# A macaron transformer kernel: bias and residual sums of the tail moved from TensorE to GpSimd, and left out of the build-time clock's stages

## The chip, the cores and the metric

The kernel runs on one core of a Trainium2 chip. The metric is the device time of one execution in microseconds (us). A core has five instruction queues that run side by side, each strictly in its own order: TensorE (PE, matrix products), VectorE (DVE), ScalarE (ACT), GpSimd (POOL) and SyncE (SP, which issues DMAs). They meet only in semaphores.

## The reference, cut to what matters

The input is 8 sequences of 512 rows by 128 features, float32. The stream `x` of each sequence goes through six layers. A routed expert layer stands first (`s = 0`), then attention (`s = 1`), then a second expert layer (`s = 2`). The last three are here called the tail:

```
x = x + 0.5 * fp6(layernorm(x))                  # called s = 3
x = x + mix(layernorm(x))                        # a gated scan, then a gated feed-forward
x = x + 0.5 * fp6(layernorm(x))                  # called s = 5

fp6(u):  out = quantized(u) @ quantized(weight).T + bias
mix(u):  u = u + scan(sigmoid, tanh of products of rmsnorm(u))
         return u + (silu(gate(rmsnorm(u))) * up(rmsnorm(u))) @ W_out.T
```

Two sums of this matter here. The first is `+ bias` in fp6, which reaches the stream halved. The second is the `u +` of mix's last line: the stream gets `x + u + product`.

## The kernel before, in words

Every sequence ("batch" `b`) has one resident tile `X[b]`, 128 partitions by 4 x 128 values (L270). The program is written by Python generators. Each yields after a stage, and a driver decides whose next stage is written down, so that the order on every engine's queue is fixed when the program is built.

The class `Clock` (L67 to L174) guesses times for that purpose. Each engine call is logged by `_Logged.noted` (L187 to L190; this is why the profile shows nearly every instruction as L190). `took` (L82) gives a guessed duration: a GpSimd operation on 512 values per partition is 0.2 + 0.0018 x 512 = 1.12 us. `account` (L100) adds a stage's operations up, moves each engine's "free" time on, and returns when the stage is over; after a GpSimd operation it adds 0.5. A generator's next stage is written only once that moment has come (`is_ready`, L143; `finish`, L164).

The order of the work: expert layer 0, then attention over the 8 batches one after another with the expert layer 2 of finished batches woven in (`drive`, L146), and last a `finish` over what remains (the last call of `tile_macaron_kernel`). The remainder is the 19 expert tiles of group 1 (batches 5, 6, 7), the gathers that combine the results of group 0 and of group 1 (`moe_combine`, L960, indirect DMAs issued by GpSimd), and the eight tails (`tail`, L1439), four in flight at most. A batch's tail starts when its gathers are done. The gathers of group 1 read what all its tiles have stored, so they start after the last of these tiles.

A tail on the engines:

- `fp6` (L1296): statistics on DVE, a power on GpSimd (`power`, L405), the normed row on ACT, quantization on DVE (`quantized`, L1249: one maximum, then six operations on 512 values), four transposes on PE (`tp_xd`), the bias product on PE (L1311), a copy of the transposes to SBUF on ACT (L1317), four products with the weight (L1320) and the sum into `X[b]` on DVE (L1326). The bias product multiplies a row of ones with the bias row and starts the accumulation in the PSUM bank `yp`.
- `mix` (L1332): statistics, powers, three products of 512 columns (`pgd`, `pgg`, `pgv`), tanh on ACT, a scan on DVE, transposes (`tp_h`), `u` completed on DVE (the tile `um_m`), the second norm, six products (`gt`, `up`), and the output. There the identity product (L1426) puts `u` into the bank `yo`, twelve products add to it, and DVE adds the bank to `X[b]` (L1437).

In attention, `roped` (L1027) makes queries and keys. It has one GpSimd sum of the same size, 128 x 512, per rope (`ta_q`, `ta_k`).

A float32 matmul of 512 columns shows as two records in the profile.

Of the kernel before, what the change touches and what calls it, by code (L numbers as in the profile page):

```python
# [9 lines left out]
F32 = mybir.dt.float32  # L10
# [3 lines left out]
ALU = mybir.AluOpType  # L14
# [3 lines left out]
P = 128  # L18
S = 512
NT = S // P  # L20
# [5 lines left out]
NGF = 3  # L26
# [40 lines left out]
class Clock:  # L67
# [32 lines left out]
    def account(self, ready, chained=True):  # L100

        end, last = ready, None
        product = ready
        for engine, op, out, args in self.log:
            took = self.took(engine, op, out, args)
            dep = end if chained and engine != last else ready
            if not chained and engine != "tensor":
                dep = product
            at = max(self.free[engine], dep) + took
            self.free[engine] = at  # L110
            if engine == "tensor":
                product = at
            end, last = (at if chained else max(end, at)) + 0.1, engine
            if op == "indirect_dma_start":
                end = at
            elif engine == "gpsimd":
                end += 0.5
        self.log.clear()
        return end
# [120 lines left out]
def kernel(  # L240
# [17 lines left out]
    nc = tc.nc  # L258
    ck = Clock(nc)
# [4 lines left out]
    cpool = ctx.enter_context(tc.tile_pool(name="const", bufs=1))  # L264
# [8 lines left out]
    X = []  # L273
    for b in range(nb):
        xt = xpool.tile([P, NT, P], F32, tag=f"x{b}", name=f"x{b}")
# [22 lines left out]
    ident = cst[:, C_ID : C_ID + P]  # L298
# [9 lines left out]
    ones = cpool.tile([P, P], F32, tag="ones", name="ones")  # L308
# [41 lines left out]
    ):  # L350
        rest_of_consts[name] = (const_tile(f"{name}_s", ap, dtype), ap)
    rope_s, wattn_s, future_s, vec_s, wq8_s, wmix_s, wout_s = (t for t, _ in rest_of_consts.values())
    bq_s = cpool.tile([P, P], F32, tag="bq_s", name="bq_s")
    half_vec = cpool.tile([P, 2], F32, tag="half_vec", name="half_vec")

    clear_rows(1)
    for t, ap in rest_of_consts.values():
        nc.sync.dma_start(out=t, in_=ap)
    nc.sync.dma_start(out=bq_s, in_=bq.partition_broadcast(P))

    nstat, vpad = [], []
    for k in range(2):
# [3 lines left out]
    def clear_for_attention():  # L366

        for t in nstat:
            ck.gpsimd.memset(t, 0.0)
            yield  # L370


        for t in vpad:
            ck.gpsimd.memset(t, 0.0)
            yield
            ck.gpsimd.memset(by_pair(t)[:, :, :, DK : DK + 1], 1.0)
            yield
        ck.gpsimd.tensor_scalar_mul(half_vec[:, 0:1], vec_s[:, V_BG : V_BG + 1], 0.5)
        ck.gpsimd.tensor_scalar_mul(half_vec[:, 1:2], vec_s[:, V_BD : V_BD + 1], 0.5)
        yield  # L380

    def by_pair(t):

        v = t.rearrange("p (a k) (y d) -> p a (k y) d", k=2, d=16)
        return v[:, :, 0:4:3, :]
# [4 lines left out]
    def bank(name):  # L390
        return p_ps.tile([P, S], F32, tag="ps", name=name)
# [5 lines left out]
    def turned(src, name):  # L397

        tp = bank(f"tp_{name}")
        for t in range(NT):  # L400
            ck.tensor.transpose(tp[:, ts(t, P)], src[:, t, :], ident)
        return tp


    def power(v, eps, name):  # L405
        rs = small.tile([P, NT], F32, tag="rs", name=f"rs_{name}")
        ck.vector.tensor_scalar_add(rs, v, eps)
        yield
        ck.gpsimd.tensor_tensor(rs, rs, mhalf[:, 0:NT], ALU.pow)
        yield  # L410
        return rs

    def moments(src, name, mv=None):
        st = small.tile([P, NT, ck.vector.BN_STATS_DIM], F32, tag="bst", name=f"st_{name}")
        if mv is None:
            mv = small.tile([P, NT, ck.vector.BN_AGGR_DIM], F32, tag="bmv", name=f"mv_{name}")
        for t in range(NT):
            ck.vector.bn_stats(out=st[:, t, :], in_=src[:, t, :])
        for t in range(NT):
            ck.vector.bn_aggr(out=mv[:, t, :], in_=st[:, t, :])  # L420
        return mv

    def normed_act(src, mv, rs, name, tag="u"):

        nb_ = small.tile([P, NT], F32, tag="nbias", name=f"nb_{tag}_{name}")
        ck.vector.scalar_tensor_tensor(nb_, mv[:, :, 0], -1.0, rs, ALU.mult, ALU.mult)
        yield
        u = wk.tile([P, NT, P], F32, tag=tag, name=f"{tag}_{name}", bufs={"um": 4, "row": 4}.get(tag, 2))
        for t in range(NT):
            ck.scalar.activation(  # L430
                u[:, t, :], src[:, t, :], AF.Identity,
                scale=rs[:, t : t + 1], bias=nb_[:, t : t + 1],
            )
        yield "product"
        return u
# [813 lines left out]
    def quantized(src, g, name, slots=None):  # L1249

        am = small.tile([P, 16], F32, tag="q_am", name=f"am_{name}")[:, 0:g]
        ck.vector.tensor_reduce(am, src, AX.X, ALU.max, apply_absolute_value=True)
        sc = small.tile([P, 16], F32, tag="q_sc", name=f"sc_{name}")[:, 0:g]
        ck.vector.tensor_scalar(sc, am, 1.0 / 7.5, 1e-30, ALU.mult, ALU.max)
        rs = small.tile([P, 16], F32, tag="q_rs", name=f"rs_{name}")[:, 0:g]
        ck.vector.reciprocal(rs, sc)
        yield
        if slots:
            yield from slots.take()

        def work(k, dtype=F32):
            t = wk.tile([P, 16, FB], dtype, tag=f"a{k}", name=f"q{k}_{name}")
            return t[:, 0:g, :]

        def along(t):
            return t.unsqueeze(2).to_broadcast([P, g, FB])

        y = work(0)
        ck.vector.tensor_tensor(y, src, along(rs), ALU.mult)

        im, t = work(1, I32), work(2)
        ck.vector.tensor_scalar(
            im, y.bitcast(I32), 0x7F800000, 0x00400000, ALU.bitwise_and, ALU.bitwise_or
        )
        m = im.bitcast(F32)
        ck.vector.tensor_scalar(m, m, 1.5, 2.0**20, ALU.max, ALU.mult)
        yield

        ck.vector.scalar_tensor_tensor(t, y, -(2.0**-21), m, ALU.add, ALU.add)
        ck.vector.tensor_tensor(t, t, m, ALU.subtract)  # L1280
        ck.vector.tensor_tensor(y, t, along(sc), ALU.mult)
        yield
        return y

    wd_t = cpool.tile([P, P], F32, tag="wd_t", name="wd_t")
# [10 lines left out]
    def fp6(b, s):  # L1296

        name = f"{s}_{b}"
        mv = moments(X[b], name)
        rs = yield from power(mv[:, :, 1], 1e-5, name)  # L1300
        u = yield from normed_act(X[b], mv, rs, name, tag="um")

        xd = yield from quantized(
            u.rearrange("p t (g k) -> p (t g) k", k=FB), S // FB, name, rounding
        )
        yield from turning.take()
        tp = turned(xd.rearrange("p (t g) k -> p t (g k)", t=NT), f"xd_{name}")
        rounding.give()

        yp = bank(f"yp_{name}")  # L1310
        ck.tensor.matmul(  # L1311
            yp.rearrange("p (t d) -> p t d", t=NT), ones[0:1, :],
            bq_s[0:1].unsqueeze(1).to_broadcast([1, NT, P]), start=True, stop=False,
        )
        yield
        xt = wk.tile([P, S], F32, tag="uT", name=f"uT_xd_{name}")
        ck.scalar.copy(xt, tp)  # L1317
        yield "product"
        for t in range(NT):
            ck.tensor.matmul(  # L1320
                yp[:, ts(t, P)], xt[:, ts(t, P)], wd_t, start=False, stop=(t == NT - 1)
            )
        turning.give()
        yield
        xb = X[b].rearrange("p t d -> p (t d)")
        ck.vector.scalar_tensor_tensor(xb, yp, 0.5, xb, ALU.mult, ALU.add)  # L1326
# [5 lines left out]
    def mix(b):  # L1332
# [19 lines left out]
        u = wk.tile([P, NT, P], F32, tag="um", name=f"um_m_{b}", bufs=4)  # L1352
# [14 lines left out]
        def gate(i, bias, half, n):  # L1367
            pg = bank(f"pg{n}_{b}")
            ck.tensor.matmul(pg, wmix_s[:, ts(i, P)], xnt, start=True, stop=True)
            t = wk.tile([P, S], F32, tag=("qm", "ka", "qa")[i], name=f"gt{n}_{b}", bufs=(2, KBUFS, 2)[i])  # L1370
            ck.scalar.activation(t, pg, AF.Tanh, bias=bias, scale=half)
            return t


        d = gate(2, half_vec[:, 1:2], 0.5, "d")
# [15 lines left out]
        uf = u.rearrange("p t d -> p (t d)")  # L1391
# [22 lines left out]
        for f in range(NGF):  # L1414
# [6 lines left out]
            ck.vector.tensor_tensor(sg, sg, pu, ALU.mult)  # L1421
            sgs.append(sg)
            yield

        yo = bank(f"yo_{b}")
        ck.tensor.matmul(yo, ident, uf, start=True, stop=False)  # L1426
        for t in range(NT):
            for f in range(NGF):
                ck.tensor.matmul(
                    yo[:, ts(t, P)], sgs[f][:, ts(t, P)], wout_s[:, f, :],  # L1430
                    start=False, stop=(t == NT - 1 and f == NGF - 1),
                )
        gating.give()
        feeding.give()
# [141 lines left out]
```

## Time and profile before

| | |
|---|---|
| three runs | 1114.25, 1116.26, 1118.13 us (median 1116.26) |
| profiled execution | 1195.04 us, of which the span of the records is 1193.3 us |
| mean granted TensorE clock in it | 0.92 |
| busy in the span | PE 995.5, DVE 683.6, ACT 494.9, POOL 472.8 us |
| the chain that ended last, by engine | PE 57%, DVE 16%, issue 7%, POOL 5%, ACT 4% |
| bias products (`yp<-bq_s,ones`) | 32 records, 23.5 us busy, the first at 932.6, the last at 1186.2 us |
| identity products (`yo<-um_m,cst`) | 16 records, 8.8 us busy, 994.7 to 1168.6 us |
| POOL sums of 128 x 512 (`ta_q`, `ta_k`) | 16, all in attention, 1266 and 1281 ns on average |
| the gathers of group 1 | POOL, 1044.7 to 1099.7 us |

The table is from one profiled execution and from three runs without a profile. A "span" counts from the first record to the last. The busy time of an engine is the union of its records. In the timelines each row is a start, a duration, the engine and the operation as output<-inputs, then shapes; brackets hold the idle time just before and who ended it. In the windows, a row is a stretch of time with the busy us of each engine and the number of instructions, then the clock that was granted to TensorE (1.00 is full speed).

### The profile page before, as it was taken

How to read it: one execution, taken by the hardware profiler on the slowest of the kernel's cores; microseconds unless marked ns; L12 is line 12 of the kernel's file. 1: busy time of each engine (PE TensorE's matmuls, PEld its weight loads, DVE VectorE, ACT ScalarE, POOL GpSimd, SP SyncE). 2: the span in 40 equal slices, each digit the busy share in tenths (PEclk: the TensorE clock that was granted, in tenths of full speed). 3: DMA queues.
4: the chain of work that ended last, by engine and by line, in shares of the span. 5: the costliest groups of instructions: out<-in, count | busy, mean ns of one | idle time of the engine just before them, and what ended most of it. 6: DMA issues, size and time to landing. Idle time of an engine off the chain costs nothing.

```text
span 1193.3 us, 20637 instructions
## 1 busy us (share of the span) xinstructions
PE 995.5 (83%) x6753; PEld 693.5 (58%) x6753; DVE 683.6 (57%) x2550; ACT 494.9 (41%) x1135; POOL 472.8 (40%) x627
## 2 busy tenths in 40 slices
PE   3351699799998998998998999999968898887795
PEld 2350598687774545555554567766957666554453
DVE  6040133355556888867676856532523775788755
ACT  1210233233354646464545444444312475544651
POOL 3647202331127658745363523214025452174210
PEclk9995799799999999989898889999979899995897
DMA  9542477487658001000000153334555550011000
GB/s 291 181 148 82 129 230 233 152 267 209 191 155 237 21 15 35 25 10 17 4 19 1 37 159 102 122 112 133 151 156 175 155 150 20 27 41 40 0 10 27
DMA packets 122363, 127.34 MB, mean 107 GB/s; under 512 B 9616, under 2 KB 103696, under 8 KB 122256
## 3 DMA queue, kind: packets, MB, share of 16 engines
q1 hardware_dynamic: 114064, 109.22, 30.4%
q0 software_dynamic: 8192, 16.79, 4.4%
q8 instruction: 54, 0.88, 0.3%
q14 instruction: 53, 0.43, 0.1%
HBM read 79.58 MB, written 46.40 MB: 106 GB/s over the span
## 4 chain that ended last, share of the span: by engine, by line
PE 57%; DVE 16%; issue 7%; another core or an unknown queue 7%; POOL 5%; ACT 4%; DMA 3%; SPq 1%; POOLq 0%; DVEq 0%; ACTq 0%
PE yp L190 13%; PE hp L190 11%; PE sa L190 9%; PE av L190 6%; PE sb L190 5%; DVE q L190 3%; POOL y L190 3%; DVE seen L190 2%; DVE x L190 2%; DVE st L190 1%; PE gt L190 1%; ACT um L190 1%; DMA y<-rows_out,at 1%; PE xp L190 1%
## 5 line engine op out<-in xcount | busy, mean ns | idle before, releaser
L190 DVE CUSTOM_DVE_ANT_0 seen<-sa,future_s 128x128 f32<-128x128 f32 (+3 forms) x512 | 225.2, 486 | 98.3 <-PE sb L190 70.5
L190 ACT ACTIVATE pm<-sb 128x512 f32<-128x512 f32 (+1 forms) x384 | 182.0, 525 | 205.0 <-PE sb L190 179.7
L190 PE MATMUL yp<-wx,hs 128*128 128x128 f32 x1472 | 207.3, 284 | 53.6 <-ACT hs L190 29.2
L190 ACT ACTIVATE hs<-hp,wx 128x256 f32<-128x256 f32 x276 | 119.8, 470 | 313.5 <-PE hp L190 188.4
L190 PEld LDWEIGHTS yp<-wx,hs 128*128 128x128 f32 x1472 | 193.1, 198 | 74.4 <-issue 34.5
L190 PE MATMUL sb<-qa,ka 32*128 32x512 f32 (+3 forms) x1024 | 222.7, 488 | 6.7 <-DVE nstat L190 4.8
L190 PE MATMUL sa<-ka,qz 32*128 32x384 f32 (+3 forms) x1024 | 211.3, 484 | 3.7 <-DVE nstat L190 2.5
L190 PE MATMUL hp<-xt,wx 128*128 128x256 f32 x736 | 204.5, 403 | 9.8 <-DVE g L190 5.3
L190 POOL TENSOR_SCALAR_AFFINE_SELECT pm<-pm 128x256 f32<-128x256 f32 x256 | 100.8, 409 | 240.3 <-ACT pm L190 229.3
L190 POOL DMA_INDIRECT y<-rows_out,at x128 | 134.9, 1054 | 137.7 <-DMA rows_out<-yo 77.9
L190 DVE TENSOR_SCALAR hs<-hp,wx 128x256 f32<-128x256 f32 x92 | 44.5, 483 | 214.6 <-ACT hs L190 196.6
L190 PEld LDWEIGHTS hp<-xt,wx 128*128 128x128 f32 x736 | 133.8, 201 | 39.7 <-issue 15.6
L190 PEld LDWEIGHTS sa<-ka,qz 32*128 32x128 f32 x1024 | 106.7, 194 | 71.8 <-issue 23.4
L190 PEld LDWEIGHTS sb<-qa,ka 32*128 32x128 f32 x1024 | 103.8, 190 | 30.5 <-DVE nstat L190 7.6
L190 POOL TENSOR_TENSOR rs<-rs,mhalf 128x4 f32<-128x4 f32 (+2 forms) x44 | 53.2, 1211 | 165.8 <-DVE rs L190 126.1
L190 PE MATMUL av<-pm,vpad 128*32 128x512 f32 (+3 forms) x1024 | 96.3, 472 | 2.8 <-POOL pm L190 2.6
L190 POOL DMA_INDIRECT by_stretch<-um,sat x64 | 64.3, 1005 | 30.6 <-DVE nt L190 13.4
L190 DVE SCALAR_TENSOR_TENSOR x<-y,g,x 128x128 f32<-128x128 f32 x128 | 47.5, 375 | 15.2 <-DMA y<-rows_out,at 11.0
L190 DVE TENSOR_TENSOR yo<-yp,wx 128x256 f32<-128x256 f32 x92 | 38.5, 418 | 29.8 <-PE yp L190 13.2
L190 POOL DMA_INDIRECT rows_in<-a,at x40 | 38.9, 971 | 28.2 <-issue 27.9
L190 PE MATMUL xp<-cst,xs 128*128 128x128 f32 x184 | 37.9, 293 | 11.5 <-DMA xs<-by_stretch 11.3
L190 ACT ACTIVATE um<-x,nb_um,rs 128x128 f32<-128x128 f32 x96 | 39.4, 484 | 17.2 <-DVE nb_um L190 11.3
(211 smaller groups left out, 1238.1 us busy)
## 6 DMA issues: line engine op xcount, KB each, us to landing
wx<-in_wexp SPq DMA_DIRECT2D x92, 578.0 KB
rows_out<-yo SPq DMA_DIRECT2D x92, 128.0 KB
by_stretch<-zero SPq DMA_DIRECT2D x8, 1280.0 KB
rows_in<-zero SPq DMA_DIRECT2D x2, 3456.0 KB
by_stretch<-zero SPq DMA_DIRECT2D x8, 768.0 KB
xs<-rows_in SPq DMA_DIRECT2D x46, 128.0 KB
xs<-by_stretch SPq DMA_DIRECT2D x46, 128.0 KB
x<-in_x SPq DMA_DIRECT2D x8, 256.0 KB
```

What stands on the lines that cost most here:

```text
L190: return call(*args, **kw)
```

## The change

- The bias of the FP6 layer leaves TensorE. The bias tile is halved once on GpSimd while the program starts; in each `fp6` GpSimd adds it to `X[b]`, written behind the transposes and ahead of ACT's copy. The bank `yp` is taken later, and each of the four weight products starts its own accumulation.
- The sum of the stream with `u` leaves TensorE. GpSimd adds `u` to `X[b]`, ahead of the output products; these start the accumulation themselves.
- In the build-time clock, a GpSimd `tensor_tensor` of more than 1.1 us still moves GpSimd's own free time, but no longer the end of the stage. By the guessed durations that holds for the 128 x 512 sums: the new ones, and the sums of `roped` in attention as well.

```diff
@@ account
             at = max(self.free[engine], dep) + took
             self.free[engine] = at
+            if engine == "gpsimd" and op == "tensor_tensor" and took > 1.1:
+                continue
             if engine == "tensor":
                 product = at
@@ constants
-    bq_s = cpool.tile([P, P], F32, tag="bq_s", name="bq_s")
+    half_bq = cpool.tile([P, P], F32, tag="half_bq", name="half_bq")
...
-    nc.sync.dma_start(out=bq_s, in_=bq.partition_broadcast(P))
+    nc.sync.dma_start(out=half_bq, in_=bq.partition_broadcast(P))
@@ clear_for_attention
+        ck.gpsimd.tensor_scalar_mul(half_bq, half_bq, 0.5)
@@ fp6
-        yp = bank(f"yp_{name}")
-        ck.tensor.matmul(
-            yp.rearrange("p (t d) -> p t d", t=NT), ones[0:1, :],
-            bq_s[0:1].unsqueeze(1).to_broadcast([1, NT, P]), start=True, stop=False,
+        ck.gpsimd.tensor_tensor(
+            X[b], X[b], half_bq.unsqueeze(1).to_broadcast([P, NT, P]), ALU.add
         )
         yield
         xt = wk.tile([P, S], F32, tag="uT", name=f"uT_xd_{name}")
         ck.scalar.copy(xt, tp)
         yield "product"
+        yp = bank(f"yp_{name}")
         for t in range(NT):
-            ck.tensor.matmul(
-                yp[:, ts(t, P)], xt[:, ts(t, P)], wd_t, start=False, stop=(t == NT - 1)
-            )
+            ck.tensor.matmul(yp[:, ts(t, P)], xt[:, ts(t, P)], wd_t, start=True, stop=True)
@@ mix
-
+        ck.gpsimd.tensor_tensor(X[b], X[b], u, ALU.add)
         yo = bank(f"yo_{b}")
-        ck.tensor.matmul(yo, ident, uf, start=True, stop=False)
         for t in range(NT):
             for f in range(NGF):
                 ck.tensor.matmul(
                     yo[:, ts(t, P)], sgs[f][:, ts(t, P)], wout_s[:, f, :],
-                    start=False, stop=(t == NT - 1 and f == NGF - 1),
+                    start=(f == 0), stop=(f == NGF - 1),
                 )
```

## The prediction

> **What bounds the kernel now.** I read the 40 slices first: the tail has PE at 0.7 to 0.9, DVE near it. Nothing removed lies ahead of 931 us, so I cut the rest by what happens in it. Columns: stretch and its length, busy us of PE, PEld, DVE, ACT, POOL, then clock, DMA share, GB/s.
>
> ```profile
> 931.00:1041.50 110.50, 99.59 (x531) 73.51 (x532) 75.62 (x238) 65.77 (x170) 41.77 (x37) 0.95 0.29 85
> 1041.50:1100.00 58.50, 44.74 (x173) 26.33 (x171) 50.76 (x148) 25.44 (x62) 35.28 (x31) 0.80 0.14 42
> 1100.00:1130.00 30.00, 21.60 (x90) 13.01 (x89) 23.90 (x77) 19.01 (x48) 5.69 (x4) 0.87 0.01 3
> 1130.00:1172.00 42.00, 40.30 (x168) 24.28 (x168) 23.04 (x57) 21.79 (x59) 5.03 (x5) 0.93 0.03 13
> 1172.00:1193.30 21.30, 7.92 (x28) 4.67 (x28) 10.02 (x25) 2.82 (x6) 1.01 (x1) 0.70 0.07 25
> ```
>
> Stretch A (to 1041.5) is the last expert tiles between tails: PE is busy 90%, it bounds. B (to 1100) is the gathers of group 1: DVE is busy 87%, POOL 60%, PE waits. C (to 1130) is mixed. D (to 1172) is PE again, 96%. E is the latency of the last batch. Next the groups by shape, from 925 us, for what is removed, and the chain in order of time (start, us, what) for how much of it the end depends on:
>
> ```profile
> L190 PE MATMUL yp<-bq_s,ones 1*128 1x512 f32 x32 | 23.5, 821 | 0.0
> L190 PE MATMUL yo<-um_m,cst 128*128 128x512 f32 x16 | 8.8, 637 | 0.0
> ```
>
> ```profile
> 1100.29 1.05 PE yp L190 x2
> ...
> 1114.92 1.37 PE yp L190 x2
> ...
> 1129.90 2.00 PE yp L190 x2
> ...
> 1148.90 3.54 PE yo L190 x26
> ...
> 1158.03 3.54 PE yo L190 x26
> ...
> 1163.90 1.05 PE yp L190 x2
> ...
> 1185.24 4.02 PE yp L190 x10
> ```
>
> The "yp x2" are bias products alone, "yo x26" holds 2 identity records, "yp x10" holds a bias.
>
> **Removed.** From PE's timeline, start to next start: a bias takes 1.05 us at full clock, 2.0 at half; an identity 0.86. In A lie five biases (2.0 at 932.64, four of 1.05) and two identities (1.52 at 994.73, 0.86 at 1032.13): 8.6 us. In B five biases (7.7) and two identities (1.7), where PE waits anyway. On the chain from 1100 on: 1.05 + 1.37 + 2.0 + 1.05 + 2.01 for biases and 2 x 0.86 for identities, 9.2 us.
>
> **Added.** 24 POOL sums, 16 biases and 8 `u`. The nearest row is the rope's sum of the same shape in attention, 1266 to 1281 ns; I take 1.27, so 30.5 us of POOL. They read `X[b]` after ACT has, which lies before the quantization, so their own operands are early. In POOL's written order seven stand before the gathers of group 1, seven among these 24 gathers, ten behind. The one-off halving of the bias stands ahead of the `half_vec` rows (128.5 us, 223 ns each for one value), where POOL is busy 24 of 100 us and nobody waits for it before 932 us: it costs nothing; uncovered some 0.4 us, between those rows and a `ka` row (773 ns for 512 values).
>
> **What a rule says against it.** VectorE's timeline in attention, against POOL's:
>
> ```profile
> 654.90 0.19 DVE L190 TENSOR_REDUCE km<-k 128x4 f32<-128x32 f32 x1
> 655.12 1.04 DVE L190 TENSOR_TENSOR oh<-cst,km 128x32 f32<-128x32 f32 x1
> ```
>
> ```profile
> 654.86 1.26 POOL L190 TENSOR_TENSOR ta_q<-ta_q,tb_q 128x512 f32<-128x512 f32 x1 [1.77 <-DVE tb_q L190]
> ```
>
> The reduce with one input ran freely beside the sum. The two-input operation, 0.19 us elsewhere in this trace (650.05), took 1.04 and ended at 656.16, when the sum did (656.12). The Trainium skill ("SBUF — State Buffer", Specifications (TRN2)) says why: DVE and GpSimd share one port pair; a DVE operation with two SBUF inputs or in a two-port mode and a GpSimd operation exclude each other, and the loser waits for the whole instruction. By that rule alone every sum may cost DVE 1.27 us, by the rows only when DVE wants such an operation. In the tail these are the quantization's six (58.6 us), the weighting of gathered rows (21.8), scan and gate product (15.3): 95.7 of 183 us DVE busy, 52%, times 87% busy in B: 45%. Bounds per sum: 0 and 1.27; below nothing is excluded, as DVE loses no work. I take 0.45 x 1.27 = 0.57. The sums in turn wait for DVE; that is inside the same bounds. A new wait comes with each: DVE's own sum into `X[b]` must wait for POOL's, and behind it on DVE stand that batch's statistics and other batches' quantization; POOL's sum is written a copy and four products earlier, 2 to 3 us, so the wait is nothing unless POOL is behind (counted in B).
>
> **Moved.** The written orders of the two programs differ. In attention the key products stand about ten rows earlier: they don't read the query sum, and PE there is at 0.9 or more, so nothing is gained or lost (bounds -2 and +2, the size of its single waits on `nstat`). The first tiles of expert layer 2 stand a few rows earlier too, where PE waited 2.38 us for `xs`; the scatters ahead of it move as much. From tile 7 of group 1 on the tail is rewoven. Up to the last tile's product the new PE order holds the same 23 pairs of `hp` but one batch less of transposes and of `pgd, pgg, pgv`: 4.0 us at 0.86 per product, moved behind. SP's loads and stores follow their tiles.
>
> **Sum.** A: 8.6 + 4.0 = 12.6 us less PE work in a stretch 90% PE; the waits for the DVE quantization stay, so I count 0.8 of it: -10. The seven sums there find DVE 68% busy and cost nothing; if DVE became the limit, 7 x 0.57 = 4.0. B: POOL's queue grows by 7 x 1.27 = 8.9 us in 58.5 with 23 free, but what is queued behind a sum are gathers and the powers that the next batches' norms need; half of it, 4.5, and 7 x 0.57 = 4.0 on DVE, partly at the same time: +6. The 4.0 us moved here hide in PE's 13.8 idle us. C to E: -9.2. But a bias also covered ACT's copy of the transposes (0.58 us at 1185.33, with its signals 0.85). In the new order the weight product of batches 4, 6, 7 of the last FP6 layer stands right behind its transposes: 3 x 0.85 = +2.6. The output products of batches 6 and 7 now stand back to back, after which DVE does both batches' statistics and quantization in a row: about 20 us from the last output product to the end, by the rows of E, where it was 18: +2. The last two bias sums fall into that quantization; with DVE in such operations nearly all the time there I take 1.4 together. So -9.2 + 2.6 + 2.0 + 1.4 = -3.2.
>
> -10 + 6 - 3.2 = -7.2 us on the profiled 1195.04 (span 1193.3 and 1.7 around it). The runs without profile took 1116.26, 0.934 of that; scaled, -6.7: **1109.5 us**.
>
> **The clock.** After PE's gap of 6.75 us up to 1128.81 the granted clock is 0.50 and the bias takes 2.07 instead of 1.12 us. The skill ("TensorE: Matmul & The Clock Gate", Part 1) puts the fall at an idle window of about 3.4 us and asks to keep PE busy. By it, taking work away lengthens gaps: one more half-clock stretch of some 4 us of work would cost 2 to 4 us. By the trace the new gaps are 0.85 us each, too short; only gaps already long are lengthened. I count nothing and keep 4 us for the range.
>
> **Rivals.**
>
> - *More gain, 1098 us.* POOL and DVE absorb the sums, and PE also bounds B. For it: PE is the chain's largest part. Then no +6 and no 1.4, and half of B's 9.4: -10 - 4.7 - 9.2 + 2.6 + 2 = -19.3, scaled -18. Against: DVE's 87% in B.
> - *No change, 1113 us.* The last tile comes earlier, but B is paced by DVE (weighting, quantization of the batches), which then gives A's 10 back: -10 + 10 - 3.2, scaled -3.0. For it: DVE idles only 7.7 us in B. Against: DVE's work on batches 0 to 4 moves forward as well.
> - *Slower, 1123 us: the port.* Every one of the 17 sums from the gathers on costs its full 1.27 us, in B through DVE's queue and at the end in the quantization: 21.6. Against it stands -10 - 9.2 + 2.6 + 2 = -14.6: +7.0, scaled +6.5. It decides from 14.6 / 17 = 0.86 us per sum. For it: the row at 655.12 lost 0.85. Against: half of DVE's time in the tail is in operations that need no lock.
> - *The sums still hold their stages* (the change doesn't do what it says): excluded in the build-time order, where ACT's copy follows the sum at once; on the chip only DVE's last sum waits for it.
>
> **Chances.** Forecast 0.40, more gain 0.16, no change 0.13, slower 0.31. A measurement of this kernel tells about 0.3%, 3.3 us, from no change: faster 0.56, within 0.13, slower 0.31. The range leaves out a tenth on each side: below 1097 (beyond the larger gain) and above 1125 (the port, plus a clock stretch of 2 us). Likeliest case alone: 1104 to 1113.
>
> **What would show it.** Bias and identity rows gone (32.3 us of PE busy), 24 POOL rows of about 1.27 us. The last tile's product about 10 us earlier than 1041. First to last gather of group 1 some 6 us longer than 55. Quantization rows of DVE stretched to a sum's end, on average 0.57 us per sum; 0.86 or more and I am wrong. After the last output product about 20 us to the end. What would make it wrong apart from that: a POOL sum stuck behind a gather that waits for its DMA, with DVE's stream sum and all behind it waiting too.

## The result and the profile after

The changed kernel took 1127.18 us (median of 5 runs, 1125.32 to 1127.94), the kernel before beside it 1114.25 (5 runs, 1110.49 to 1118.13). The ratio is 1.0116, 95% interval 1.0088 to 1.0145: about 13 us slower, where 7 us faster was forecast. The profiled execution took 1127.34 us (span 1125.5). The profiled execution of before, 1195.04 us, was far slower than that kernel's other runs: its first rope sum came at 253.88 us, in a second profile of the same kernel at 186.21, and 18 us more went by its end. So the stages are compared below with that second profile, the run `e1_before_again` (1109.01 us, span 1107.3; the median of its runs is 1114.06).

The four windows of the kernel before in that second profile; columns as in the prediction's windows. The first ends, as the prediction's stage A does, just ahead of the first gather of group 1; the second is its B, the third C and D, the fourth E:

```profile
849.00:955.40 106.40, 96.63 (x531) 71.92 (x532) 75.44 (x238) 65.75 (x170) 41.51 (x37) 0.98 0.30 88
955.40:1013.90 58.50, 44.68 (x173) 26.36 (x172) 50.66 (x149) 25.42 (x62) 35.20 (x31) 0.80 0.14 42
1013.90:1085.90 72.00, 62.02 (x257) 37.59 (x255) 46.84 (x133) 40.80 (x106) 10.72 (x9) 0.91 0.02 9
1085.90:1107.30 21.40, 7.91 (x28) 4.67 (x28) 10.10 (x25) 2.82 (x6) 1.01 (x1) 0.70 0.07 25
```

The same stages of the changed kernel:

```profile
849.00:952.80 103.80, 90.26 (x506) 70.18 (x505) 79.23 (x224) 58.00 (x147) 51.00 (x44) 0.95 0.32 97
952.80:1026.00 73.20, 42.34 (x177) 28.52 (x176) 65.62 (x168) 34.88 (x88) 48.55 (x42) 0.76 0.13 37
1026.00:1103.50 77.50, 58.95 (x243) 36.65 (x241) 49.53 (x125) 38.76 (x101) 21.20 (x17) 0.88 0.02 8
1103.50:1125.50 22.00, 5.30 (x25) 4.18 (x24) 13.72 (x32) 4.47 (x10) 4.13 (x4) 0.64 0.06 24
```

Read the DVE column (the third busy time, with the number of instructions behind it). In B it rises from 50.66 to 65.62 us, in the third stage from 46.84 to 49.53 although it has eight instructions fewer there. PE's busy time over the four falls from 211 to 197 us, by less than the 30 us of the products that are gone (the others last longer, see the clock further down), and the stages get longer from B on: 58.5 to 73.2, 72.0 to 77.5, 21.4 to 22.0.

Next some of DVE's groups by shape from 810 us to the end, before (second profile) and then after. The numbers behind the bar are busy us, then mean ns of one; behind the second bar stands the idle time ahead of the group:

```profile
L190 DVE SCALAR_TENSOR_TENSOR x<-y,g,x 128x128 f32<-128x128 f32 x64 | 21.9, 348 | 8.1 <-DMA y<-rows_out,at 7.0
L190 DVE TENSOR_TENSOR_SCAN scan<-gtd,gtg 128x512 f32<-128x512 f32 x8 | 9.8, 1224 | 0.8
L190 DVE TENSOR_SCALAR q<-q 128x512 int32<-128x512 int32 x16 | 7.1, 442 | 0.6
L190 DVE TENSOR_REDUCE am<-um 128x16 f32<-128x512 f32 x16 | 10.9, 679 | 4.5 <-ACT um L190 4.5
```

```profile
L192 DVE SCALAR_TENSOR_TENSOR x<-y,g,x 128x128 f32<-128x128 f32 x64 | 30.3, 480 | 10.0 <-DMA y<-rows_out,at 9.0
L192 DVE TENSOR_TENSOR_SCAN scan<-gtd,gtg 128x512 f32<-128x512 f32 x8 | 11.9, 1486 | 0.7
L192 DVE TENSOR_SCALAR q<-q 128x512 int32<-128x512 int32 x16 | 10.7, 670 | 0.6
L192 DVE TENSOR_REDUCE am<-um 128x16 f32<-128x512 f32 x16 | 10.9, 680 | 7.8 <-ACT um L192 7.7
```

The work is the same, the counts are the same, and three of the four forms last longer: the weighting of gathered rows 348 to 480 ns, the scan 1224 to 1486, the integer step of the quantization 442 to 670. The reduce, with one input, does not change (679, 680). Neither does an operation whose second input lies in PSUM, such as `silu<-silu,up` (683, 681 ns). What they last longer by lies under GpSimd's new rows, of which there are 24 of 1.33 us on average:

```profile
L192 POOL TENSOR_TENSOR x<-x,half_bq 128x512 f32<-128x512 f32 x16 | 21.3, 1332 | 9.3 <-ACT um L192 9.1
L192 POOL TENSOR_TENSOR x<-x,um_m 128x512 f32<-128x512 f32 x8 | 10.5, 1322 | 0.1
```

Three of them in GpSimd's timeline, and then DVE's timeline at the same moments:

```profile
963.28 1.28 POOL L192 TENSOR_TENSOR x<-x,um_m 128x512 f32<-128x512 f32 x1
...
965.75 1.28 POOL L192 TENSOR_TENSOR x<-x,half_bq 128x512 f32<-128x512 f32 x1
...
979.73 1.28 POOL L192 TENSOR_TENSOR x<-x,half_bq 128x512 f32<-128x512 f32 x1
```

```profile
963.02 2.08 DVE L192 SCALAR_TENSOR_TENSOR x<-y,g,x 128x128 f32<-128x128 f32 x2
...
965.80 2.32 DVE L192 TENSOR_TENSOR_SCAN scan<-gtd,gtg 128x512 f32<-128x512 f32 x1
...
979.56 2.21 DVE L192 TENSOR_SCALAR q<-q 128x512 int32<-128x512 int32 x2
981.80 0.69 DVE L192 SCALAR_TENSOR_TENSOR q<-q,q 128x512 f32<-128x512 f32 x1
```

Two weightings take 0.70 us elsewhere; those at 963.02 took 2.08, and the sum beside them ended at 964.56, just ahead of their end at 965.10. The scan at 965.80 took 2.32 instead of 1.22. The two quantization steps at 979.56 took 2.21 instead of 0.89, and behind them `q<-q,q` started only at 981.80. Each of these three sums cost DVE its whole length or more than 1 us of it.

### The profile page after: what moved, and what is told of

Same layout as the page of the kernel before. It is cut to its first block, busy times and chain, and to the rows that moved or that the text cites. A ratio compares the mean times of both kernels' runs of the same rounds, so it can differ in the third digit from the quotient of the medians.

```text
span 1125.5 us, 20568 instructions
## 1 busy us (share of the span) xinstructions
PE 960.6 (85%) x6705; PEld 677.6 (60%) x6705; DVE 711.2 (63%) x2550; ACT 496.7 (44%) x1135; POOL 507.7 (45%) x652
## 4 chain that ended last, share of the span: by engine, by line
PE 56%; DVE 18%; issue 8%; POOL 7%; ACT 5%; DMA 5%; SPq 1%; POOLq 0%; ACTq 0%; DVEq 0%
PE yp L192 12%; PE hp L192 12%; PE sa L192 9%; PE av L192 6%; PE sb L192 5%; DVE q L192 3%; POOL y L192 3%; DVE seen L192 2%; DVE x L192 2%; DMA y<-rows_out,at 2%; DVE st L192 1%; PE lp L192 1%; PE xp L192 1%; ACT um L192 1%; PE yo L192 1%
## 5 line engine op out<-in xcount | busy, mean ns | idle before, releaser
L192 PE MATMUL sb<-qa,ka 32*128 32x512 f32 (+3 forms) x1024 | 225.0, 487 | 8.7 <-DVE nstat L192 7.1
L192 PE MATMUL yp<-wx,hs 128*128 128x128 f32 x1472 | 198.4, 278 | 4.1 <-DVE hs L192 4.1
L192 PEld LDWEIGHTS yp<-wx,hs 128*128 128x128 f32 x1472 | 186.5, 193 | 23.3 <-issue 11.8
L192 PE MATMUL hp<-xt,wx 128*128 128x256 f32 x736 | 196.8, 392 | 0.0
L192 PEld LDWEIGHTS hp<-xt,wx 128*128 128x128 f32 x736 | 130.2, 196 | 20.9 <-issue 4.6
L192 POOL DMA_INDIRECT by_stretch<-um,sat x64 | 64.0, 1001 | 33.0 <-DVE nt L192 13.8
L192 DVE SCALAR_TENSOR_TENSOR x<-y,g,x 128x128 f32<-128x128 f32 x128 | 57.9, 455 | 20.5 <-DMA y<-rows_out,at 18.4
L192 PE MATMUL xp<-cst,xs 128*128 128x128 f32 x184 | 37.4, 287 | 28.2 <-DMA xs<-by_stretch 14.8
L192 DVE COPY xt<-xp 128x256 f32<-128x256 f32 x92 | 38.3, 416 | 25.1 <-PE xp L192 25.1
L192 PEld LDWEIGHTS xp<-cst,xs 128*128 128x128 f32 x184 | 26.0, 146 | 39.5 <-issue 27.2
```

Source lines behind the costliest of these rows:

```text
L192: return call(*args, **kw)
```

## The experiments

All times are medians; one run of each kernel was profiled. The kernel before was run again beside each of the three groups of kernels (medians 1113.09 beside e1 to e4, 1113.29 beside e5 to e8, 1113.81 us beside e9 to e12), and the ratios are to these runs. "Old order" and "new order" mean that every instruction that is not edited keeps the place that it has in the kernel before or in the changed kernel; where an operation is left out, the build-time clock is still told of it. Kernels named "none", "scratch", "fills", "powers" and "two sums" leave the bias and `u` out of the stream.

| run | order | in place of the 24 products | us | ratio to before, 95% |
|---|---|---|---|---|
| e1 | old | the products (kernel before) | 1114.06 | 1.0009, 0.9988 to 1.0031 |
| e3 | old | nothing | 1103.55 | 0.9907, 0.9877 to 0.9937 |
| e2 | old | sums into `X[b]` | 1122.00 | 1.0079, 1.0050 to 1.0108 |
| e4 | new | nothing | 1107.84 | 0.9950, 0.9934 to 0.9965 |
| changed kernel | new | sums into `X[b]` | 1127.18 | 1.0116, 1.0088 to 1.0145 |
| e5 | new | sums on unused tiles | 1123.72 | 1.0111, 1.0078 to 1.0143 |
| e6 | new | fills of 1.25 us | 1113.10 | 1.0009, 0.9990 to 1.0029 |
| e7 | new | powers of 5 values, 1.2 to 1.3 us | 1107.58 | 0.9949, 0.9934 to 0.9965 |
| e12 | new | two sums on unused tiles each | 1141.60 | 1.0241, 1.0213 to 1.0270 |
| e8 | old | bias product in bf16, identity kept | 1105.79 | 0.9942, 0.9918 to 0.9967 |
| e11 | old | bias product in bf16, sums of `u` | 1109.61 | 0.9961, 0.9942 to 0.9980 |
| e9 | before plus the clock's line | the products | 1113.84 | 1.0017, 0.9995 to 1.0040 |
| e10 | changed kernel without that line | sums into `X[b]` | 1137.77 | 1.0215, 1.0187 to 1.0242 |

### Order and sums taken apart: e1 to e4

e1 is the kernel before, unedited. e2 puts the sums into the order of before:

```diff
-        ck.tensor.matmul(yo, ident, uf, start=True, stop=False)
+        ck.log.append(("tensor", "matmul", yo, (yo, ident)))
+        nc.gpsimd.tensor_tensor(X[b], X[b], u, ALU.add)
```

and the same for the bias; `nc.gpsimd` is the engine without the log, so the clock sees the old product. e3 is e2 without the sums. e4 is the changed kernel without them:

```diff
-        ck.gpsimd.tensor_tensor(X[b], X[b], u, ALU.add)
+        ck.log.append(("gpsimd", "tensor_tensor", X[b], (X[b],)))
```

> The kernel before, unchanged, for a profile beside its own time: the profiled execution of before took 1195.04 us against a median of 1114.25, so its stages can't be set beside those of the changed kernel. Every theory expects a ratio of 1.000 within 0.003. What tells them apart is its profile: if the port theory holds, attention starts and ends within 3 us of the changed kernel's (rope sum at 186.7, power of batch 7 at 783.3 us) and the 13 us arise behind the gathers of group 1; if the loss lies in attention's new order, the power of batch 7 comes 5 us or more ahead of 783.

> The whole change of operations in the written order of before: the GpSimd sums stand where the two PE products stood, and the build-time clock is told of the products as before. Port theory: the sums cost DVE about 0.9 us each here too, 24 x 0.9 = 21.8 us of DVE in the tail, so the time is 1120 to 1130 us, ratio 1.005 to 1.015. Order theory (the loss comes from the new order): faster than before, 1100 to 1110, ratio 0.985 to 0.997.

> The written order of before with both PE products left out and no sums in their place: the FP6 bias and the stream's sum with u are missing from the result. It prices the products alone. Both theories: faster than before. Port theory: by the 16.8 us of them that stood on the chain, less what then waits for ACT's copy, 8 to 14 us, 1100 to 1106. If the products were only cover for waits: within 3 us of before.

> The changed kernel with its written order and its build-time clock, but the 24 sums left out: the FP6 bias and the stream's sum with u are missing from the result. It prices the sums in their own order. Port theory: 15 to 22 us faster than the changed kernel, 1105 to 1112. Order theory: within 4 us of the changed kernel, 1123 to 1128, and 15 us or more slower than the same operations in the old order.

Measured: 1114.06, 1122.00, 1103.55 and 1107.84 us. The products are worth 9.5 us (1113.1 to 1103.55). The sums cost 18.5 us in the old order (1103.55 to 1122.00) and 19.3 in the new one (1107.84 to 1127.18), that is 0.77 to 0.81 us for each of the 24. The new order alone costs 4.3 us (1103.55 to 1107.84). The three add up: -9.5 + 19.3 + 4.3 = +14.1 against 12.9 measured. The sums are the cause of the loss; the order by itself takes back about half of what leaving out the products gains.

### What about a sum costs: e5, e6, e7

Three readings of a sum were left: DVE's own sum into `X[b]` waits for it; GpSimd's queue is longer, with gathers and powers behind it; DVE is held up while it runs. In e5 the sum reads and writes tiles that nobody else uses in the tail. In e6 a fill of the same length stands in its place, in e7 a power of two inputs of five values:

```diff
@@ e5 (the other sum: nstat[0], nstat[1])
+        nc.gpsimd.tensor_tensor(
+            vpad[0].rearrange("p a d -> p (a d)")[:, 0:S].rearrange("p (t d) -> p t d", t=NT),
+            nstat[0], half_bq.unsqueeze(1).to_broadcast([P, NT, P]), ALU.add,
+        )
@@ e6
+        nc.gpsimd.memset(vpad[0].rearrange("p a d -> p (a d)")[:, 0:1377], 0.0)
@@ e7
+        nc.gpsimd.tensor_tensor(nstat[0][:, 0, 0:5], mhalf[:, 0:5], mhalf[:, 5:10], ALU.pow)
```

> The written order is that of the changed kernel. Each of its 24 sums is still one GpSimd sum of 128x512, at the same place in GpSimd's queue, but it adds two tiles that nobody else uses in the tail and writes a third one: bias and u are left out of the result. GpSimd's time is kept and no instruction of another engine waits for the sum any more. If GpSimd's time or its hold on VectorE costs: about 1127 us, as the changed kernel. If the wait of VectorE's sum into X[b] for GpSimd's sum costs: about 1108, as with the sums left out. I expect 1125 to 1128.

> The same order. Each of the 24 sums is replaced by a GpSimd fill of 1377 values per partition of an unused tile, 1.27 us by the rows of the fills of 512 (0.55 us) and 2048 values (1.83 us): GpSimd's queue is as long, nothing is read from SBUF, nobody waits; bias and u are left out. If the longer queue costs (gathers and powers behind the sums): about 1127 us. If it is the hold on VectorE by an operation that reads SBUF twice: near 1108 us. I expect 1108 to 1113, since the added VectorE time of the changed kernel, 0.91 us per sum, explains its loss by itself.

> The same order. Each of the 24 sums is replaced by a GpSimd power of two inputs of 5 values per partition, some 1.2 us by the rows of 4 values (1.03 us) and 8 (1.71 us), on unused values: two SBUF inputs, but 5 of them instead of 512; bias and u are left out. If VectorE is held for the whole of a GpSimd instruction of two inputs, whatever it reads: about 1125 us. If the hold follows what is read and written: near 1108 us. I have no ground to prefer one; a middle value would mean part of each.

Measured: 1123.72, 1113.10 and 1107.58 us. e5 has nearly the ratio of the changed kernel (1.0111 and 1.0116; its median is 3.5 us lower, a little under what I expected): the wait of DVE's sum for GpSimd's is not the cause, or a small part of the 19 us, 3.5 by the medians and 0.6 by the ratios. Nor do the queues meet only in semaphores: no instruction waits for these sums, and DVE is held up all the same (23.1 us, in the table below). e7 has a GpSimd queue that is 30.9 us longer than e4's and takes the same time (0.9949 and 0.9950, each within 0.0016): the longer queue is not the cause either, and what it costs the gathers and powers behind it does not show. Its rows, GpSimd's and then two of DVE's groups from 810 us on:

```profile
L1314 POOL TENSOR_TENSOR nstat<-mhalf 128x5 f32<-128x5 f32 x16 | 21.5, 1341 | 0.3
```

```profile
L192 DVE SCALAR_TENSOR_TENSOR x<-y,g,x 128x128 f32<-128x128 f32 x64 | 21.9, 348 | 5.7 <-DMA y<-rows_out,at 4.7
L192 DVE TENSOR_SCALAR q<-q 128x512 f32<-128x512 f32 x16 | 6.9, 432 | 0.6
```

DVE's means are no longer than before (348, and 459 for the second). So a GpSimd instruction of two inputs does not hold DVE by being there for 1.3 us. That it is the amount of data which counts is the nearest reading; it is not shown by itself, since a power is also another operation than a sum. The fill lies between, 5.3 us over e4, just above what I expected, and the DVE groups of its run say which operations a fill holds up:

```profile
L192 DVE SCALAR_TENSOR_TENSOR x<-y,g,x 128x128 f32<-128x128 f32 x64 | 21.9, 349 | 7.2 <-DMA y<-rows_out,at 6.3
L192 DVE TENSOR_SCALAR q<-q 128x512 f32<-128x512 f32 x16 | 10.2, 637 | 0.5
```

The weighting with its inputs in SBUF is untouched (349 ns), and the quantization step with one input has gone from 432 to 637 ns. The timelines of this run show the same for single rows, GpSimd first, then DVE:

```profile
971.71 1.27 POOL L1314 MEMSET vpad<- 128x1377 f32 x1
...
993.94 1.27 POOL L1314 MEMSET vpad<- 128x1377 f32 x1
```

```profile
970.87 2.39 DVE L192 TENSOR_SCALAR q<-q 128x512 int32<-128x512 int32 x2
...
992.99 1.38 DVE L192 SCALAR_TENSOR_TENSOR x<-y,g,x 128x128 f32<-128x128 f32 x4
```

Four weightings ran at full speed (1.38 us for four), the last of them beside the fill at 993.94; two quantization steps that met the fill at 971.71 took 2.39 us, 0.89 elsewhere. The Trainium skill ("SBUF — State Buffer", section "Who interferes with whom") draws this line: a DVE operation with two SBUF inputs is in conflict only with a GpSimd operation that reads SBUF, one in a two-port mode with any. The fill agrees, if `TENSOR_SCALAR` ran in such a mode, which no row names. The page has this in that section, not in the one that the prediction names, and the prediction left out that a fill spares the operations with two inputs. It also says that the pair is held for the whole instruction; for the sums the rows above agree, for the power of five values (1.34 us, DVE's groups 0.4 us longer in all) they don't, and the measurement decides.

The prices can be checked against each other. Take each DVE group of the tail, its mean less its mean in e4, times its count, and add up; that is the DVE time that was held up. Beside it stands the time of the kernel over that of the same order with nothing in place:

| run | DVE time held up, us | time over "nothing", us |
|---|---|---|
| e7, powers | 0.4 | -0.3 |
| e6, fills | 5.8 | 5.3 |
| e2, sums, old order | 19.3 (20.2 less e3's 0.9) | 18.5 |
| e5, sums on unused tiles | 23.1 | 15.9 |
| changed kernel, sums | 23.4 | 19.3 |
| e12, two sums each | 35.9 | 33.8 |

Most of what DVE loses in this tail, the kernel loses, in some runs all of it. The changed kernel's 23.4 us are 17.3 in operations with two SBUF inputs and 6.0 in `TENSOR_SCALAR`s with one.

### The dose, and another way: e8, e11, e12

e12 is e5 with each sum written twice. e8 is the kernel before with a cheaper product: the bias is split once into three bf16 rows that add up to it, and the product runs in bf16:

```diff
+        nc.gpsimd.memset(bq16, 0.0)
+        for k in range(3):
+            row = slice(32 * k, 32 * k + 1)
+            for _ in range(k):
+                nc.gpsimd.tensor_copy(bq16[row], bq_s[row])
+                nc.gpsimd.tensor_tensor(bq_s[row], bq_s[row], bq16[row], ALU.subtract)
+            nc.gpsimd.tensor_copy(bq16[row], bq_s[row])
+        nc.gpsimd.memset(bq_s.bitcast(BF16)[:, 0:P], 1.0)
...
-            yp.rearrange("p (t d) -> p t d", t=NT), ones[0:1, :],
-            bq_s[0:1].unsqueeze(1).to_broadcast([1, NT, P]), start=True, stop=False,
+            yp.rearrange("p (t d) -> p t d", t=NT), bq_s.bitcast(BF16)[:, 0:P],
+            bq16.unsqueeze(1).to_broadcast([P, NT, P]), start=True, stop=False,
```

e11 is e8 with the second half of the change: the sums of `X[b]` with `u` on GpSimd in place of the identity products.

> The kernel before and its written order, with one edit: the bias product stays on TensorE but takes bf16 operands. The bias is split once into three bf16 rows that add up to it, and ones of bf16 stand against them. By the records a float32 product of 512 columns takes 1.05 us[...], so 16 x 0.8 = 12.8 us less TensorE work. Leaving out all of bias and identity products (25.2 us of work at full clock) made 9.5 us, so with this share of it: 5 us, about 1108 us, if the price of a bias is its TensorE time. If the price is the slot of the product between transposes and weight products: no change, 1113.

> The bf16 bias product on TensorE, in the order of before, and of the change only the 8 sums of X[b] with u on GpSimd in place of the identity products. With 0.8 us for each sum they cost 6.4 us; the identity products removed are 8 x 0.86 us of TensorE's work, 2.6 us by the share in which the removed products came back (9.5 of 25.2 us). So 1105.8 + 6.4 - 2.6 = 1109.6 us. If sums with u are cheaper than sums with the bias, since they stand where VectorE is less busy: 1103 to 1106.

> The order of the changed kernel, with two sums on unused tiles in a row at each of the 24 places; bias and u are left out. One such sum at each place cost 16 us over none (1123.72 against 1107.84). If each holds VectorE by about the same: 1140 us. If VectorE works through what can run beside a sum and only the first of two hurts: about 1124. If GpSimd's queue, longer by 61 us in the tail, now bounds the gathers as well: above 1145.

Measured: 1105.79, 1109.61 and 1141.60 us. e12 adds 17.9 us to e5 for the second 24 sums, after 15.9 for the first: in time each costs about the same, as expected. DVE was held up only 12.8 us more by them, so some 5 us came about in another way, which these runs do not show. e8 is faster than both kernels. Its bias rows, which were 32 records and 22.1 us busy in e1:

```profile
L1321 PE MATMUL yp<-bq,bq_s 128*128 128x512 bf16 x16 | 7.1, 443 | 0.0
```

15 us of PE's busy time are gone (12.8 expected) and 7.5 us of the kernel's (1113.29 to 1105.79; 6.5 by the ratio, 3.7 to 9.1 by its interval), about half; the 5 us expected lie within. e11 took 3.8 us more than e8 by the medians, and its time is the one expected (1109.6). Its eight sums held DVE up by 4.9 us more than in e8, 0.6 each. By the ratios e11 is only 2.1 us slower than e8, and their intervals overlap: that this half of the change loses by itself is likely, not shown.

### The clock's line: e9, e10

e9 is the kernel before with nothing but the clock's line (`continue` for a large GpSimd sum); e10 is the changed kernel with those two lines taken out.

> The kernel before with one line more, the clock's: a large GpSimd sum no longer holds up the end of a stage. Bias and u stay on TensorE, no instruction is added or removed; the key products in attention stand earlier, as in the changed kernel, and what follows is rewoven. With all sums left out, the changed kernel's order was 4.3 us slower than the order of before (1107.84 against 1103.55). If that price lies in this line's effect on attention: about 1117 us. If it lies in the tail that was rewoven around the sums: about 1113, no change. I lean to the first, since the start of the tail was some 3 us later in the profiles of the changed order.

> The changed kernel without the clock's line: the 24 sums are on GpSimd and count in the clock as any other operation, so attention is ordered as before and the tail is woven around stages that end later. If the loss is VectorE's time under the sums, 0.8 us each, it is here too: 1113 - 9.5 + 19 = 1122 us with the order of before, up to 1127 with a worse one. If the clock's line is what made the changed kernel slow: about 1113 or less.

Measured: 1113.84 us, no change that shows, and 1137.77 us. For e9 the value I did not lean to came out. So the 4.3 us of the new order lie more likely in the tail that was rewoven around the sums than in attention; as the interval of e9's ratio reaches 1.0040, this is not certain. e10 is 10.6 us slower than the changed kernel, beyond both values that I gave. In its profile the last gather of group 1 ends 15 us earlier than in the changed kernel (1010.5 against 1025.8 us), but the part behind takes 125 us instead of 100. So the line made the change less bad: in the order written without it more of the tails lies behind the gathers (200 DVE instructions against 157). Why such an order loses more there than it gains ahead was located by these profiles and not taken apart further.

## Why the prediction was wrong

**The step that failed is the price of a sum**, "I take 0.45 x 1.27 = 0.57", with nothing for the seven sums in A. The prediction put 7.4 us on all 24 sums (+6 in B, with GpSimd's queue, and 1.4 at the end). They took 19.3 us, 0.81 each, and held DVE up for 23.4 us, 0.97 each, beyond the 0.86 that it had named as its sign of being wrong. With 19.3 in place of 7.4 its -7.2 would read +4.7: the sign turns on this step. The second miss is the gain without sums: -14.6 stood for the missing products and the new order together, -5.2 was measured (-9.5 and +4.3).

The measured steps, from one profile each: the time of the first gather of group 0, then up to the end of the last expert tile's product, from there to the first gather of group 1, to the end of its last gather, and to the end of the span.

| us | to 1st gather, group 0 | to last tile (A) | gap | gathers of group 1 (B) | rest (C to E) | span |
|---|---|---|---|---|---|---|
| e1, before | 823.1 | 132.4 | 3.1 | 54.9 | 93.7 | 1107.3 |
| e3, products left out | 820.5 | 128.7 | 3.1 | 53.0 | 89.4 | 1094.7 |
| e4, and the new order | 827.1 | 119.8 | 3.0 | 61.6 | 94.6 | 1106.1 |
| changed kernel | 827.0 | 125.8 | 3.2 | 69.7 | 99.7 | 1125.5 |

The profiled executions of e1 and e3 were 5 and 7 us faster than the medians of their kernels. Counted from the first gather on, the steps from row to row are -10.0, +4.8 and +19.5 us, close to those of the medians (-9.5, +4.3, +19.3); a difference of a few us in one column stays uncertain.

- **A, "8.6 + 4.0 = 12.6 us less PE work ... -10": right in sum by luck, and then half lost.** Products and order brought the last tile forward by 12.6 us (132.4 to 119.8), but the products gave 3.7 of it, where 8.6 stood, and the order 8.9, where 4.0 stood. "The seven sums there find DVE 68% busy and cost nothing" failed: DVE's rows there last 8.2 us longer than in e4, 1.17 for each sum, and the last tile came 6.0 us later (119.8 to 125.8), so 6.6 us earlier in all. PE's waits for DVE from 827 us to the last tile, in e4 and then in the changed kernel (us in total, times, longest):

```profile
PE tp_h L192 <- DVE scan L192: 4.4, 3, 4.1
PE tp_xd L192 <- DVE q L192: 1.8, 1, 1.8
PE yp L192 <- DVE hs L192: 0.2, 1, 0.2
```

```profile
PE tp_h L192 <- DVE scan L192: 5.2, 3, 4.1
PE yp L192 <- DVE hs L192: 3.8, 2, 2.5
PE tp_xd L192 <- DVE q L192: 3.2, 3, 2.0
```

They grew from 6.4 to 12.2 us, by nearly what the last tile lost: a DVE that is free on average is not free at the moment when PE needs it.
- **Why 0.57 was too low.** The estimate took the share of DVE's time in operations that can be held up, as if a sum fell on one instant. It covers 1.27 us, two or three DVE instructions, and since DVE works in order, the first one that can be held up stops all behind it until the sum ends; the rows at 963.02 and 979.56 show it. In B the rows of DVE last 10.8 us longer than in e4 under eight sums, 1.35 each, the upper bound of 1.27 and a little more (the windows, 55.52 and 65.62 us, cut off the last of these rows); behind B it is 4.5 us under nine, 0.5 each. The row of attention that the prediction showed at 655.12 (1.04 us for 0.19) was the right one to size it by.
- **B, "half of it, 4.5" for GpSimd's queue: failed.** No cost of it shows (e7). **"These 4.0 us moved here hide in PE's 13.8 idle us": failed.** The new order with no sums made B 8.6 us longer, about what it had taken from A. The window of B in e3 and then in e4:

```profile
949.10:1005.70 56.60, 36.30 (x160) 24.57 (x159) 50.72 (x150) 25.65 (x62) 34.96 (x31) 0.76 0.15 43
```

```profile
946.70:1011.80 65.10, 40.83 (x178) 27.67 (x177) 55.52 (x167) 34.84 (x88) 38.99 (x33) 0.79 0.14 42
```

PE's part grew by 4.5 us, as the prediction had it. But seventeen DVE instructions and 4.8 us came with it into a stage in which DVE was busy 50.72 of 56.6 us. The step followed the moved products on PE and not the DVE work of the same batch. B came out at +14.8 us (-1.9 products, +8.6 order, +8.1 sums), where +6 stood.
- **C to E, "-9.2 + 2.6 + 2.0 + 1.4 = -3.2": failed in three terms.** Leaving the products out gave -4.3 and not -9.2: less than half of the 9.2 us seen on the chain came back. The order cost +5.2, of which 2.6 + 2.0 stood there. The 2.0 rested on a wrong reading: from the last output product to the end it took 21.4 us before, not 18 (1171.9 to 1193.3 in the profile of before; 21.4 in e1 too), and 22.0 in the changed kernel, so the +5.2 arose elsewhere. The sums cost +5.1, where 1.4 stood for the last two and nothing for the others there.
- **The clock, put at nothing because the new gaps are too short.** The windows from the first gather to the end, in e1, e3, e4 and the changed kernel:

```profile
823.10:1107.30 284.20, 234.00 (x1140) 161.34 (x1138) 199.22 (x589) 144.08 (x365) 106.72 (x96) 0.91 0.21 65
820.50:1094.70 274.20, 208.38 (x1092) 155.00 (x1091) 198.70 (x589) 143.81 (x366) 106.69 (x96) 0.88 0.22 68
827.05:1106.10 279.05, 212.69 (x1101) 156.20 (x1099) 198.02 (x589) 145.20 (x367) 110.35 (x96) 0.89 0.22 66
827.00:1125.50 298.50, 216.37 (x1081) 157.52 (x1079) 220.44 (x589) 144.09 (x364) 142.06 (x120) 0.86 0.20 62
```

With the products gone and PE waiting longer, the granted clock fell from 0.91 to 0.86, and the products that all four kernels have lasted, counted by groups as for DVE, 12.8 us more in sum in the changed kernel than in e1 (6.7 more than in e4). How much of this reached the end is not separated here, so a part of the 19.3 us of the sums may have come by way of it. DVE's 589 instructions took 22.4 us more than in e4.
- **What held.** The halving of the bias (561 ns at 112.7 us) moved nothing: the first rope sum came at 186.68 us, 186.21 in e1. The new order of attention, taken at 0 with 2 us either way, shows no cost in e9, within its interval (-0.6 to +4.5 us). The scaling by 0.934 had no ground in the tail, whose stages from B on last the same in both profiles of the kernel before (58.5, 72.0 and 21.3 or 21.4 us); it changed the forecast by 0.5 us.
- **The rival "the port"** named the mechanism and gave 1123. Its size for the sums (21.6 us, 19.3 measured) was about right because two errors met: 17 sums at full price, where 24 took part at 0.81. It lacked the price of the new order and took the products' gain too high.

## What to carry to other kernels

Before work is moved from TensorE to GpSimd, look at what VectorE does at that moment. Here a GpSimd sum of 1.33 us that streams SBUF held up VectorE's operations with two SBUF inputs and its `TENSOR_SCALAR`s for 0.97 us on average, for its whole length (1.35) where VectorE was 90% busy and for 1.17 where it was 76% busy, and most of that reached the kernel's time. Size such a price by a row in which the two meet, not by shares of time. A product on TensorE that costs too much may be made cheaper in place: the 16 bias products in bf16 took 7.1 us of TensorE instead of 22.1, and with no other instruction of the tail moved the kernel became 6 to 7 us faster (4 to 9 by the interval). When an order is rewoven, follow a batch's work on every engine into the stage that receives it, not on the one that it was taken from.

## What was not expected of the hardware

- A GpSimd power on two inputs of 5 values (1.34 us) held no VectorE operation that shows (0.4 us in 24); a fill of 1.25 us held only those with one SBUF input in `TENSOR_SCALAR` (432 to 637 ns), not those with two (348, 349); a sum of 128x512 held both.
- A held VectorE row shows as a longer row, not as idle time ahead of it: the weightings' idle share hardly moved (8.1 to 10.0 us for all 64) while their busy time rose from 21.9 to 30.3 us.
- The kernel before has a wide spread without any edit: 1101.95 to 1121.58 us in the 43 runs beside e5 to e8.
